# Projecting q and k of a head pair in one step, with ScalarE emptying the banks, in a convolution and attention hybrid with routed experts

## The chip, the cores and the metric

The kernel runs on one core of a Trainium2 chip. The metric is the device time in microseconds of one execution. The engines named below are TensorE (PE, with its weight loads as PEld), VectorE (DVE), ScalarE (ACT), GpSimd (POOL) and SyncE (SP).

## What is computed

The input is 8 images of 256 channels and 32 x 32 positions, so 1024 tokens of 256 features each, in float32. Three layers follow one another:

```
layer 0:  qkv = x @ w_qkv + b_qkv           8 heads of 64
          attn = softmax over i of (q_i . k_j) / 8
          x = attn @ v @ w_out + b_out + x
layer 1a: n = layer_norm(t);  t = t + softmax(n W^T n^T) n
layer 1b: n = layer_norm(t);  t = t + n + sum over the 2 best of 8 experts of
          gate * (gelu(n @ w1[e] + b1[e]) @ w2[e] + b2[e])
```

## The kernel before

The eight images are called batches. For each, `layer0` runs the attention of layer 0, `attend` the attention of layer 1, `normed` the normalisation and the router's logits. The tokens of batches 0 to 6 are scattered by expert into a DRAM table (`dispatch`) and go through `experts` in blocks after `layer0` of batch 7; batch 7 goes through all experts in `dense`.

The change lies in the head loop of `layer0`. The 8 heads form 4 pairs g. Of each pair the loop takes 8 blocks j of 128 keys, so there are 32 steps, written (g,j) below. A step consists of these parts, and TensorE gets them in this order:

- `score` makes the scores of a block of keys against 1024 queries, for head h and half n of the queries, as two 64 x 64 matmuls (psc, L399). Each head's scores take one pair of PSUM banks from the pool `ps_big`, which has three pairs. Of head 1 the second half is left to the next step.
- `first_max` and `soften` (L414, L426, L436): VectorE finds the maximum of each half, ScalarE takes the exponential with its sum. `divide` scales the values with the sums (L447).
- `gather_values` multiplies exponentials with values (po, L467) for the block two steps back (LAG), in two turns of four 64 x 64 matmuls. After the last block of a pair ScalarE copies the two accumulators to `res` (L486). The accumulators of the next pair are in the same two banks.

The first pair's q and k come from `Begin`, before the loop. Those of pair g+1 are made inside the loop by `project` (L300): four 128 x 128 matmuls into a pair of banks for q at one step and for k at another, emptied by VectorE with bias and scale (L290, in `evict`; the ScalarE form is L287). The places are listed in `PROJECT`: (0,3) and (0,5), then (g,1) and (g,5) for g = 1 and 2. At the step (3,2), the one change of pair that has no projection before it, the flag `late` puts the first turn of value products behind the scores.

The routing of the previous batch (`gates` and `dispatch`, on VectorE, with two counting matmuls, L752 and L753, into a third pair of banks `pcn`) is a generator. `share` resumes it, each time up to its next `yield`. It is resumed at step (0,0), at the places of `PROJECT`, and from (1,6) on at each step for one scatter (L804, GpSimd). In batch 0 there is nothing to route. `plan` computes on VectorE which block belongs to which expert (L830 to L879), once, behind the last eviction of batch 7 in VectorE's order, which is at (2,5).

The order on each engine is drawn up by a scheduler from dependencies; `issue_after` adds an edge on one engine alone, without a wait, and `declare_no_dep` removes a dependency that a pair of banks would give.

Of the kernel before, what the change touches and what calls it, by code (L numbers as in the profile page):

```python
# [10 lines left out]
F32 = mybir.dt.float32  # L11
I32 = mybir.dt.int32
AF = mybir.ActivationFunctionType
# [6 lines left out]
def kernel(  # L20
# [23 lines left out]
    nc = tc.nc  # L44
    P = 128
    B, C, S = x.shape
    E, D, FF = w1.shape
# [3 lines left out]
    NCC = C // P  # L51
    NT = S // P
    NH2 = S // 512
    NPAIR = INNER // P
# [20 lines left out]
    def big(name):  # L75

        return ps_big.tile([P, 1024], F32, tag="big", name=name)
# [216 lines left out]
    def project(b, xT, g, t, scalar=False):  # L294

        pq = big(f"pqk_{b}_{g}_{t}")
        dst = two.tile([P, S], F32, tag=f"qk{t}", name=f"qk{t}_{b}_{g}")
        for n in range(NH2):
            for cc in range(NCC):
                mm = nc.tensor.matmul(  # L300
                    pq[:, ts(n, 512)],
                    wqkv[:, cc, t, ts(g, P)],
                    xT[:, cc, ts(n, 512)],
                    start=(cc == 0),
                    stop=(cc == NCC - 1),
                )
                if n > 0:

                    tc.declare_no_dep(mm.ins, evicted[b, g, t].ins, reason="the other bank")
            evicted[b, g, t] = evict(dst[:, ts(n, 512)], pq[:, ts(n, 512)], g, t, scalar)  # L310
        return dst

    class Begin:


# [54 lines left out]
    def layer0(b, xT, begun, routing):  # L370
# [9 lines left out]
        steps = [(g, j) for g in range(NPAIR) for j in range(NT)]  # L380
        LAG = 2

        PROJECT = [(0, 3), (0, 5)]
        PROJECT += [(g, j) for g in range(1, NPAIR - 1) for j in (1, 5)]
        FIRST_SCATTER = PROJECT[3]
        seconds, turned = {}, {}

        relay = nc.gpsimd if b == 0 else nc.sync
        pss, firsts, nmaxes, exps, sums, vss = {}, {}, {}, {}, {}, {}
        po = None  # L390

        def score(at, h, n):
            g, j = steps[at]
            q, k = qks[g]
            if n == 0:
                pss[at, h] = big(f"psc_{b}_{g}_{j}_{h}")
            r = slice(h * DK, (h + 1) * DK)
            for c in range(2):
                mm = nc.tensor.matmul(  # L399
                    pss[at, h][ts(c, DK), ts(n, 512)],  # L400
                    k[r, j * P + c * DK : j * P + (c + 1) * DK],
                    q[r, ts(n, 512)],
                    start=True,
                    stop=True,
                )
                if n == 1:

                    tc.declare_no_dep(mm.ins, firsts[at, h].ins, reason="the other bank")
# [7 lines left out]
            )  # L416
            nmaxes[at, h] = nmax

        def soften(at, h):

            g, j = steps[at]
            ps = pss.pop((at, h))
            if h == 0:
                sums[at] = small.tile([P, 2], F32, tag="sums", name=f"sums_{b}_{g}_{j}")
            nmax = small.tile([P, 1], F32, tag="nmax", name=f"nmax_{b}_{g}_{j}_{h}")
            seconds[h] = nc.vector.tensor_scalar(  # L426
                scrap,
                ps[:, ts(1, 512)],
                -1.0,
                nmaxes.pop((at, h)),  # L430
                ALU.mult,
                ALU.min,
                accum_out=nmax,
            )
            ex = expp.tile([P, 1024], F32, tag="exps", name=f"ex_{b}_{g}_{j}_{h}")
            nc.scalar.activation(  # L436
                ex, ps, AF.Exp, bias=nmax, scale=1.0, accum_out=sums[at][:, h : h + 1]
            )
            exps[at, h] = ex

# [14 lines left out]
        def gather_values(at, turn):  # L455


            nonlocal po
            g, j = steps[at]
            if j == 0 and turn == 0:  # L460
                po = [acc(f"po_{b}_{g}_{n}") for n in range(NH2)]
            past = dict(turned)
            for half in range(2):
                keys = ts(half, DK)
                n = (half + turn) % 2
                for h in range(2):
                    mm = nc.tensor.matmul(  # L467
                        po[n][ts(h, DK), :],
                        vss[at][keys, h, :],
                        exps[at, h][keys, ts(n, 512)],  # L470
                        start=(j == 0 and turn == 0),
                        stop=(j == NT - 1 and turn == 1),
                    )
                    if h == 0 and (j > 0 or turn > 0):
                        tc.add_manual_dep(mm.ins, past[1 - half].ins.name, BEHIND)

                turned[half] = relay.nop()
                tc.add_manual_dep(turned[half].ins, mm.ins.name, BEHIND)
            if turn == 0:
                return mm  # L480
            vss.pop(at)
            for h in range(2):
                exps.pop((at, h))
            if j == NT - 1:
                for n in range(NH2):
                    nc.scalar.copy(res[:, g, ts(n, 512)], po[n])  # L486
            return mm

        last = len(steps) - 1
        def share(behind=None):  # L490

            try:
                routing.send(behind)
            except StopIteration:
                pass

        for at in range(last + LAG + 1):
            g, j = steps[min(at, last)]

            late = at > LAG and steps[at - LAG][1] == 0 and (g, j - 1) not in PROJECT  # L500
            if at <= last:
                score(at, 0, 0)
            if 0 < at <= last + 1:
                score(at - 1, 1, 1)
                soften(at - 1, 1)
            if at >= LAG and not late:
                gather_values(at - LAG, 0)
            if at <= last:

                with tc.issue_after(seconds[1].ins) if 1 in seconds else nullcontext():  # L510
                    first_max(at, 0)
                score(at, 0, 1)
                score(at, 1, 0)
                soften(at, 0)
                with tc.issue_after(seconds[0].ins):
                    ahead = divide(at - 1) if at > 0 else seconds[0]
                with tc.issue_after(ahead.ins):
                    first_max(at, 1)
            elif at == last + 1:
# [136 lines left out]
    def gates(b, lT):  # L656
# [82 lines left out]
    def dispatch(b, n2, l, group):  # L739
# [13 lines left out]
        nc.tensor.matmul(pcn[:, NT * E : 2 * NT * E], ones, flat, start=True, stop=True)  # L753
# [59 lines left out]
    def plan(group):  # L813


        with tc.issue_after(evicted[B - 1, NPAIR - 1, 1].ins):
            return plan_blocks(group)

    def plan_blocks(group):
        n, nb, cap = group.n, group.nb, group.cap  # L820
        counts = group.counts
        steps = cap // BR
# [56 lines left out]
        nc.vector.tensor_copy(w_at[:, :nb], hi)  # L879

        group.first = first
        return row_at, w_at

    def places(group):

# [22 lines left out]

    def experts(group):
        n = group.n  # L910
        row_at, w_at = plan(group)

        wbs_x = [*wbs, one.tile([P, WROW], F32, tag="v", name="wb_x")]

# [343 lines left out]
```

## Time and profile before

| | us |
|---|---|
| median of three runs | 2485.18 (2483.05 to 2487.45) |
| profiled execution, whole time | 2485.58 |
| profiled execution, span on the core | 2483.9 |
| granted TensorE clock, mean | 0.988 |
| head loop of batch 3, window 788 to 930: TensorE busy | 140.16 of 142 |
| the same window: VectorE, ScalarE busy | 115.26, 82.54 |

The profile is of one execution. Its timeline has the start and the duration of each instruction in microseconds from the start of the span, then engine, line, operation, output and inputs, and in brackets how long the engine had stood idle and what released it. Rows of single instructions are merged into xN, some matmul records are missing, and a matmul in float32 shows as two records. The releaser is inferred from semaphores, so a name in brackets is the event that came last and need not be the cause.

### The profile page before, as it was taken

To read this page: it belongs to the slowest core of one execution; us is meant where nothing else is said; L and a number is where in the kernel's file an instruction comes from. 1 tells how busy PE (TensorE), PEld (TensorE's weight loads), DVE (VectorE), ACT (ScalarE), POOL (GpSimd) and SP (SyncE) were. 2 spreads that over 40 slices of the span, in tenths; PEclk is the share of its full clock that TensorE was granted. 3 is DMA by queue.
4 is the path that set the end of the run, shared out by engine and by line. 5 is a ranking of instruction groups with operands and counts; after the bars stand their busy time and mean duration, and the time that the engine had idled before them with its cause. 6 is when DMAs were issued, how large, how long until landed. Compare 5 with 4: busy or idle time off the path is not lost.

```text
span 2483.9 us, 37112 instructions
## 1 busy us (share of the span) xinstructions
PE 2405.0 (97%) x14015; PEld 1310.7 (53%) x14015; DVE 1564.7 (63%) x3738; ACT 888.4 (36%) x1491; POOL 388.6 (16%) x383
## 2 busy tenths in 40 slices
PE   9999999999999999999999999999999999997789
PEld 3356434653465346533653365336633788865456
DVE  5874687468746875687568845885588643335434
ACT  2641355135512561255125612561255222211212
POOL 0000001000100010002000200020002354443461
PEclk9999999999999999999999999999999999998899
DMA  7993001000100000000000000000001466652352
GB/s 282 385 370 76 35 10 43 1 18 10 43 1 18 10 28 16 18 8 29 18 17 6 31 17 18 4 33 1 18 4 62 130 213 224 212 161 85 116 185 81
DMA packets 82556, 188.22 MB, mean 76 GB/s; under 512 B 13993, under 2 KB 23881, under 8 KB 80585
## 3 DMA queue, kind: packets, MB, share of 16 engines
q1 hardware_dynamic: 57368, 118.65, 13.4%
q0 software_dynamic: 25008, 67.20, 8.7%
q8 instruction: 111, 1.82, 0.3%
q14 instruction: 69, 0.56, 0.1%
HBM read 100.49 MB, written 110.90 MB: 85 GB/s over the span
## 4 chain that ended last, share of the span: by engine, by line
PE 78%; DVE 4%; ACT 2%; issue 1%; another core or an unknown queue 1%; DMA 1%; ACTq 0%; POOL 0%; DVEq 0%; SPq 0%; POOLq 0%
PE psc L399 15%; PE po L467 15%; PE py L617 8%; PE pqk L300 8%; PE ps L591 6%; PE ph L945 4%; PE pr L557 4%; PE pe L970 4%; PE pv L336 3%; PE pdy L1152 2%; PE px L576 2%; PE pdh L1128 2%; PE pa L610 2%; ACT ex L436 1%
## 5 line engine op out<-in xcount | busy, mean ns | idle before, releaser
L436 ACT ACTIVATE ex<-psc,nmax 128x1024 f32<-128x1024 f32 x512 | 570.2, 1114 | 472.2 <-DVE scrap L426 371.3
L399 PE MATMUL psc<-qk,qk 64*64 64x512 f32 x4096 | 568.2, 593 | 7.3 <-ACT ex L436 7.2
L467 PE MATMUL po<-ex,vs 64*64 64x512 f32 x4096 | 558.4, 591 | 5.4 <-DVE vs L447 4.1
L426 DVE TENSOR_SCALAR_CACHE_REDUCE scrap<-psc,nmax 128x512 f32<-128x512 f32 x512 | 384.5, 751 | 99.4 <-PE psc L399 72.4
L414 DVE TENSOR_REDUCE nmax<-psc 128x1 f32<-128x512 f32 x512 | 350.8, 685 | 12.0 <-PE psc L399 12.0
L399 PEld LDWEIGHTS psc<-qk,qk 64*64 64x64 f32 x4096 | 174.8, 132 | 299.5 <-issue 148.9
L467 PEld LDWEIGHTS po<-ex,vs 64*64 64x64 f32 x4096 | 166.7, 132 | 285.1 <-issue 97.6
L617 PE MATMUL py<-n,aT 128*128 128x256 f32 x1024 | 244.4, 393 | 18.0 <-DVE aT L612 13.2
L300 PE MATMUL pqk<-xT,wqkv 128*128 128x512 f32 x512 | 235.0, 602 | 5.4 <-ACT ex L436 5.2
L617 PEld LDWEIGHTS py<-n,aT 128*128 128x128 f32 x1024 | 195.9, 195 | 83.3 <-DVE aT L612 51.0
L804 POOL DMA_INDIRECT rows<-n,d_at x112 | 108.9, 972 | 828.6 <-DVE nmax L414 824.3
L591 PE MATMUL ps<-nT,xa 128*128 128x512 f32 x512 | 236.5, 592 | 0.0
L602 ACT ACTIVATE ex<-ps,nmax 128x1024 f32<-128x1024 f32 x64 | 71.3, 1114 | 354.7 <-DVE nmax L599 345.7
L734 POOL TENSOR_TENSOR t<-t,n 128x2048 f32<-128x2048 f32 x8 | 36.2, 4531 | 947.0 <-issue 680.5
L622 DVE SCALAR_TENSOR_TENSOR t<-py,rs,t 128x256 f32<-128x256 f32 x64 | 31.0, 484 | 233.9 <-PE py L617 207.8
L300 PEld LDWEIGHTS pqk<-xT,wqkv 128*128 128x128 f32 x512 | 93.3, 190 | 133.3 <-issue 92.8
L591 PEld LDWEIGHTS ps<-nT,xa 128*128 128x128 f32 x512 | 93.6, 190 | 79.9 <-issue 73.6
L1017 POOL DMA_INDIRECT yk<-y,yat x112 | 115.6, 1032 | 126.9 <-DVE o L1049 77.5
L336 PE MATMUL pv<-wqkv,xT 128*128 128x512 f32 x256 | 119.7, 597 | 0.0
L599 DVE TENSOR_REDUCE nmax<-ps 128x1 f32<-128x1024 f32 x64 | 78.3, 1224 | 59.1 <-PE ps L591 59.1
L557 PE MATMUL pr<-wo,res 128*128 128x256 f32 x512 | 111.8, 379 | 0.0
L290 DVE TENSOR_SCALAR qk<-pqk,b_qk 128x512 f32<-128x512 f32 x100 | 73.8, 748 | 59.6 <-PE pqk L300 59.6
(191 smaller groups left out, 2430.5 us busy)
## 6 DMA issues: line engine op xcount, KB each, us to landing
rows<-wb SPq DMA_DIRECT2D x7, 8192.0 KB
y<-yb SPq DMA_DIRECT2D x63, 256.0 KB
xT<-in_x_dram SPq DMA_DIRECT2D x7, 1024.0 KB
sums<-t SPq DMA_DIRECT2D x7, 1024.0 KB
o<-sums SPq DMA_DIRECT2D x7, 1024.0 KB
out_dram<-oT SPq DMA_DIRECT2D x14, 512.0 KB
wpack<-in_L_ffn_w_dram SPq DMA_DIRECT2D x4, 1024.0 KB
wb<-in_L_ffn_w_dram SPq DMA_DIRECT2D x16, 256.0 KB
```

The source lines that it names most:

```text
L300: mm = nc.tensor.matmul(pq[:, ts(n, 512)], wqkv[:, cc, t, ts(g, P)], xT[:, cc, ts(n, 512)], start=(cc == 0), stop=(cc == NCC - 1),)
L336: nc.tensor.matmul(pv, self.xT[:, cc, ts(i, P)], wqkv[:, cc, 2, :], start=(cc == 0), stop=(cc == NCC - 1),)
L399: mm = nc.tensor.matmul(pss[at, h][ts(c, DK), ts(n, 512)], k[r, j * P + c * DK : j * P + (c + 1) * DK], q[r, ts(n, 512)], start=True, stop ...
L414: firsts[at, h] = nc.vector.tensor_reduce(nmax, pss[at, h][:, ts(0, 512)], AX.X, ALU.max, negate=True)
L426: seconds[h] = nc.vector.tensor_scalar(scrap, ps[:, ts(1, 512)], -1.0, nmaxes.pop((at, h)), ALU.mult, ALU.min, accum_out=nmax,)
L436: nc.scalar.activation(ex, ps, AF.Exp, bias=nmax, scale=1.0, accum_out=sums[at][:, h : h + 1])
L467: mm = nc.tensor.matmul(po[n][ts(h, DK), :], vss[at][keys, h, :], exps[at, h][keys, ts(n, 512)], start=(j == 0 and turn == 0), stop=(j == ...
L557: nc.tensor.matmul(pr[:, :C], res[:, g, ts(i, P)], wo[:, g, :], start=(g == 0), stop=(g == NPAIR - 1))
L591: nc.tensor.matmul(psc[:, ts(n, 512)], xa[:, ec, ts(i, P)], nT[:, ec, ts(n, 512)], start=(ec == 0), stop=(ec == NCC - 1),)
L617: nc.tensor.matmul(py[:, :D], aT[:, ts(m, P)], n1[:, m, :], start=(m == 0), stop=(m == NT - 1))
L804: scatter = nc.gpsimd.indirect_dma_start(out=view[:, :], out_offset=bass.IndirectOffsetOnAxis(ap=ats[k][:, i : i + 1], axis=0), in_=n2[:, ...
L1017: nc.gpsimd.indirect_dma_start(out=yk[:, i, k, :], out_offset=None, in_=self.group.y[:, :], in_offset=bass.IndirectOffsetOnAxis(ap=ats[k][ ...
```

## The change

A new `project_pair` makes q and k of the next pair in one step, eight matmuls into one pair of banks: q in the first and second bank, then k in the first and second, each bank emptied by ScalarE before it is written again. The dependencies between different banks are removed. `PROJECT` has three places: (0,3), (1,1) and (2,1).

The routing loses three of its `yield`s. At (0,3) the whole of `gates` runs, and the counting matmuls go into the first of the pair's banks, behind k's last matmul; the scores and the value products of the step after are ordered behind them. At (1,1) comes all the rest up to the first scatter, and the scatters run from (1,2) on. `plan` is called at (2,1) of batch 7.

The second maximum becomes a function of its own. `late` is gone; at (3,1) the flag `early` puts the exponential of head 0 behind the two copies to `res` in ScalarE's order.

```diff
+    def project_pair(b, xT, g):
+        pq = big(f"pqk_{b}_{g}")
+        dsts, left = [], []
+        for t in range(2):
+            dst = two.tile([P, S], F32, tag=f"qk{t}", name=f"qk{t}_{b}_{g}")
+            for n in range(NH2):
+                for cc in range(NCC):
+                    mm = nc.tensor.matmul(
+                        pq[:, ts(n, 512)],
+                        wqkv[:, cc, t, ts(g, P)],
+                        xT[:, cc, ts(n, 512)],
+                        start=(cc == 0),
+                        stop=(cc == NCC - 1),
+                    )
+                    for at, ins in left:
+                        if at != n:
+                            tc.declare_no_dep(mm.ins, ins, reason="the other bank")
+                left.append((n, evict(dst[:, ts(n, 512)], pq[:, ts(n, 512)], g, t, True).ins))
+            dsts.append(dst)
+        return dsts, pq, mm
...
-        PROJECT = [(0, 3), (0, 5)]
-        PROJECT += [(g, j) for g in range(1, NPAIR - 1) for j in (1, 5)]
-        FIRST_SCATTER = PROJECT[3]
+        PROJECT = [(0, 3), *((g, 1) for g in range(1, NPAIR - 1))]
...
-                for n in range(NH2):
-                    nc.scalar.copy(res[:, g, ts(n, 512)], po[n])
+                copied = [nc.scalar.copy(res[:, g, ts(n, 512)], po[n]) for n in range(NH2)]
...
-            late = at > LAG and steps[at - LAG][1] == 0 and (g, j - 1) not in PROJECT
+            early = at > LAG and j == 1 and (g, j) not in PROJECT
             if at <= last:
-                score(at, 0, 0)
+                with tc.issue_after(counted.ins) if counted else nullcontext():
+                    score(at, 0, 0)
             if 0 < at <= last + 1:
-                score(at - 1, 1, 1)
+                with tc.issue_after(counted.ins) if counted else nullcontext():
+                    score(at - 1, 1, 1)
+                second_max(at - 1, 1)
                 soften(at - 1, 1)
-            if at >= LAG and not late:
-                gather_values(at - LAG, 0)
+            if at >= LAG:
+                with tc.issue_after(counted.ins) if counted else nullcontext():
+                    gather_values(at - LAG, 0)
+                counted = None
...
                 score(at, 0, 1)
                 score(at, 1, 0)
-                soften(at, 0)
+                second_max(at, 0)
+                if not early:
+                    soften(at, 0)
...
-            if late:
-                gather_values(at - LAG, 0)
             if at >= LAG:
                 array = gather_values(at - LAG, 1)
-            project_now = at <= last and (g, j) in PROJECT
-            if at <= last and (project_now or (g, j) > FIRST_SCATTER):
+            if early:
+                with tc.issue_after(copied[0].ins), tc.issue_after(copied[1].ins):
+                    soften(at, 0)
+            if at <= last and (g, j) in PROJECT:
                 with tc.issue_after(firsts[at, 1].ins), tc.issue_after(array.ins):
                     share(firsts[at, 1])
-            if project_now:
-                if len(qks) == g + 1:
-                    qks.append([])
-                qks[g + 1].append(project(b, xT, g + 1, len(qks[g + 1])))
+                    pair, pq, mm = project_pair(b, xT, g + 1)
+                qks.append(pair)
+                if g == 0:
+                    with tc.issue_after(mm.ins), tc.issue_after(firsts[at, 1].ins):
+                        counted = share(pq)
+                if b == B - 1 and (g, j) == PROJECT[-1]:
+                    with tc.issue_after(firsts[at, 1].ins):
+                        plan(groups[0])
+            elif at <= last and (g, j) > PROJECT[1]:
+                share(firsts[at, 1])
...
-        yield
         top2, hot2 = first_of_max(rest, "g_2")
...
-        yield
-        pcn = big(f"pcn_{b}")
+        pcn = yield
...
+        yield counted
...
-        yield
         for k in range(2):
```

The pair's matmuls are L322 in the changed kernel, the counting matmuls L792 and L793, the exponentials L461, the evictions still L287.

More of the change, by code (lines that the diff above doesn't have):

```diff
@@ L389, in layer0 @@
         pss, firsts, nmaxes, exps, sums, vss = {}, {}, {}, {}, {}, {}
-        po = None
+        po, copied, counted = None, None, None
         def score(at, h, n):
@@ L417, in first_max, with second_max @@
             nmaxes[at, h] = nmax
-        def soften(at, h):
+        def second_max(at, h):
             g, j = steps[at]
-            ps = pss.pop((at, h))
-            if h == 0:
-                sums[at] = small.tile([P, 2], F32, tag="sums", name=f"sums_{b}_{g}_{j}")
             nmax = small.tile([P, 1], F32, tag="nmax", name=f"nmax_{b}_{g}_{j}_{h}")
@@ L427, in soften @@
                 scrap,
-                ps[:, ts(1, 512)],
+                pss[at, h][:, ts(1, 512)],
                 -1.0,
-                nmaxes.pop((at, h)),
+                nmaxes[at, h],
                 ALU.mult,
@@ L434, in soften @@
             )
+            nmaxes[at, h] = nmax
+        def soften(at, h):
+            g, j = steps[at]
+            if h == 0:
+                sums[at] = small.tile([P, 2], F32, tag="sums", name=f"sums_{b}_{g}_{j}")
             ex = expp.tile([P, 1024], F32, tag="exps", name=f"ex_{b}_{g}_{j}_{h}")
             nc.scalar.activation(
-                ex, ps, AF.Exp, bias=nmax, scale=1.0, accum_out=sums[at][:, h : h + 1]
+                ex,
+                pss.pop((at, h)),
+                AF.Exp,
+                bias=nmaxes.pop((at, h)),
+                scale=1.0,
+                accum_out=sums[at][:, h : h + 1],
             )
@@ L455, in gather_values @@
         def gather_values(at, turn):
-            nonlocal po
+            nonlocal po, copied
             g, j = steps[at]
@@ L492, in share @@
             try:
-                routing.send(behind)
+                return routing.send(behind)
             except StopIteration:
-                pass
+                return None
         for at in range(last + LAG + 1):
             g, j = steps[min(at, last)]
-            late = at > LAG and steps[at - LAG][1] == 0 and (g, j - 1) not in PROJECT
+            early = at > LAG and j == 1 and (g, j) not in PROJECT
             if at <= last:
-                score(at, 0, 0)
+                with tc.issue_after(counted.ins) if counted else nullcontext():
+                    score(at, 0, 0)
             if 0 < at <= last + 1:
-                score(at - 1, 1, 1)
+                with tc.issue_after(counted.ins) if counted else nullcontext():
+                    score(at - 1, 1, 1)
+                second_max(at - 1, 1)
                 soften(at - 1, 1)
-            if at >= LAG and not late:
-                gather_values(at - LAG, 0)
+            if at >= LAG:
+                with tc.issue_after(counted.ins) if counted else nullcontext():
+                    gather_values(at - LAG, 0)
+                counted = None
             if at <= last:
@@ L748, in dispatch @@
         nc.vector.tensor_add(both, hots[0], hots[1])
-        yield
-        pcn = big(f"pcn_{b}")
+        pcn = yield
         flat = both.rearrange("p i e -> p (i e)")
         nc.tensor.matmul(pcn[:, : NT * E], before, flat, start=True, stop=True)
-        nc.tensor.matmul(pcn[:, NT * E : 2 * NT * E], ones, flat, start=True, stop=True)
+        counted = nc.tensor.matmul(pcn[:, NT * E : 2 * NT * E], ones, flat, start=True, stop=True)
         cn = small.tile([P, 2, NT, E], F32, tag="d_cn", name=f"d_cn_{b}", bufs=1)
         nc.vector.tensor_copy(cn.rearrange("p t i e -> p (t i e)"), pcn[:, : 2 * NT * E])
+        yield counted
         per = small.tile([P, E, NT], F32, tag="d_per", name=f"d_per_{b}", bufs=1)
@@ L813, in plan @@
     def plan(group):
-        with tc.issue_after(evicted[B - 1, NPAIR - 1, 1].ins):
-            return plan_blocks(group)
-    def plan_blocks(group):
         n, nb, cap = group.n, group.nb, group.cap
@@ L881, in plan_blocks @@
         group.first = first
-        return row_at, w_at
+        group.where = row_at, w_at
     def places(group):
@@ L910, in experts @@
         n = group.n
-        row_at, w_at = plan(group)
+        row_at, w_at = group.where
         wbs_x = [*wbs, one.tile([P, WROW], F32, tag="v", name="wb_x")]
```

## The prediction

> **What bounds the kernel now.** I read the page's busy shares, then the chain, then the chip's timeline of single steps, because the answer must come from places where TensorE waits.
>
> ```profile
> PE 2405.0 (97%) x14015; PEld 1310.7 (53%) x14015; DVE 1564.7 (63%) x3738; ACT 888.4 (36%) x1491; POOL 388.6 (16%) x383
> L399 PE MATMUL psc<-qk,qk 64*64 64x512 f32 x4096 | 568.2, 593 | 7.3 <-ACT ex L436 7.2
> L290 DVE TENSOR_SCALAR qk<-pqk,b_qk 128x512 f32<-128x512 f32 x100 | 73.8, 748 | 59.6 <-PE pqk L300 59.6
> ```
>
> TensorE is the bound: busy 97%, 78% of the chain. Only time in which it stands still or works inefficiently inside the eight head loops (142 us each) is to be had; the matmuls themselves stay. Since an overlapping busy row hides small gaps, I use a clock of my own: the distance from the first exponential (h = 0) of one step to that of the next. A plain step takes 3.43 us, almost everywhere. What a step takes beyond that, and beyond its extra matmuls, is loss. Batch 3, a step with one projection:
>
> ```profile
> 862.04 1.11 ACT L436 ACTIVATE ex<-psc,nmax 128x1024 f32<-128x1024 f32 x1 [0.35 <-DVE rs L445]
> 865.37 0.30 PEld L300 LDWEIGHTS pqk<-xT,wqkv 128*128 128x128 f32 x2 [0.81 <-ACT ex L436]
> 865.47 1.11 ACT L436 ACTIVATE ex<-psc,nmax 128x1024 f32<-128x1024 f32 x1 [0.34 <-DVE rs L445]
> 867.39 0.75 DVE L290 TENSOR_SCALAR qk<-pqk,b_qk 128x512 f32<-128x512 f32 x1 [1.01 <-PE pqk L300]
> 869.00 0.21 PEld L399 LDWEIGHTS psc<-qk,qk 64*64 64x64 f32 x8 [0.76 <-issue]
> 872.69 1.11 ACT L436 ACTIVATE ex<-psc,nmax 128x1024 f32<-128x1024 f32 x1 [0.48 <-DVE rs L445]
> ```
>
> 862.04 to 865.47 is the plain step, 865.47 to 872.69 (7.22 us) the step with a projection. The weight loads inside it start every 0.43 us, eight of them: 3.44 us of work. So 7.22 - 3.43 - 3.44 = **0.35 us** is lost at each entry and exit. It looks like a wait for ScalarE's exponential (0.81), but that one began at 863.92 and took 1.11, and its accumulator was read by 865.12, 0.25 us before the load: the gap lies where the 64*64 tiles turn into 128*128 and back.
>
> The dearer places, found by the same clock:
>
> ```profile
> 828.90 1.11 ACT L436 ACTIVATE ex<-psc,nmax 128x1024 f32<-128x1024 f32 x1 [0.35 <-DVE rs L445]
> 830.16 0.30 PEld L300 LDWEIGHTS pqk<-xT,wqkv 128*128 128x128 f32 x2 [0.84 <-ACT ex L436]
> 837.48 1.11 ACT L436 ACTIVATE ex<-psc,nmax 128x1024 f32<-128x1024 f32 x1 [0.48 <-DVE rs L445]
> ```
>
> Step (1,1) takes 8.58, which is 1.36 more than 7.22: the counting matmuls (loads at 828.80 and 829.02) took the free pair of banks, and the projection waits for the exponential that began at 828.90 to give back its own. Seven batches have this; batch 0 routes nothing.
>
> ```profile
> 900.52 1.11 ACT L436 ACTIVATE ex<-psc,nmax 128x1024 f32<-128x1024 f32 x1 [0.35 <-DVE rs L445]
> 901.62 1.06 ACT L486 COPY res<-po 128x512 f32<-128x512 f32 x2
> 903.89 1.11 ACT L436 ACTIVATE ex<-psc,nmax 128x1024 f32<-128x1024 f32 x1
> 908.47 1.11 ACT L436 ACTIVATE ex<-psc,nmax 128x1024 f32<-128x1024 f32 x1 [0.48 <-DVE rs L445]
> ```
>
> Steps (3,1) and (3,2), the one change of pair without a projection: 7.95 for 6.87, 1.08 lost, in every batch.
>
> ```profile
> 1887.55 1.11 ACT L436 ACTIVATE ex<-psc,nmax 128x1024 f32<-128x1024 f32 x1 [0.34 <-DVE rs L445]
> 1896.50 1.11 ACT L436 ACTIVATE ex<-psc,nmax 128x1024 f32<-128x1024 f32 x1 [1.45 <-DVE rs L445]
> 1902.24 1.09 PE L399 MATMUL psc<-qk,qk 64*64 64x512 f32 x8 [2.55 <-ACT ex L436]
> 1902.47 1.11 ACT L436 ACTIVATE ex<-psc,nmax 128x1024 f32<-128x1024 f32 x1 [0.28 <-DVE rs L445]
> ```
>
> Batch 7, (2,5) and (2,6): 8.95 and 5.97 instead of 7.22 and 3.43, together 4.3 lost, because the plan's VectorE work (L830 to L879) sits among the second maxima.
>
> ```profile
> 299.86 1.11 ACT L436 ACTIVATE ex<-psc,nmax 128x1024 f32<-128x1024 f32 x1 [7.61 <-PE po L467]
> ```
>
> Batch 1 alone: pair 0 takes 42.94 us where batch 2 takes 36.74, so 6.2 lost. Its value products stand behind the projection in TensorE's order, and ScalarE waits for them (7.61) to free a buffer of exponentials.
>
> **What the Trainium skill says.** (1) TensorEngine Tiling (Array Packing), Key Properties: "Mode switching requires drain". The trace agrees; the price here is the 0.35. (2) ScalarE: Activation LUTs, Table sets: identity and copy are in every set, so an eviction between exponentials needs no load. The trace agrees for the copies of L486, which stand between exponentials without one; for identity there it shows nothing. (3) PSUM — Partial Sum Buffer, PSUM bank collisions: engines on different banks run clean, on one bank they must be kept apart. Agrees: loads go on every 0.43 us while VectorE empties the first bank.
>
> **The change part by part.**
>
> *A. Six projections become three pairs.* 24 entries fewer in eight batches, 24 x 0.35 = **8.4**. Does the shared pair of banks take it back? Count from the pair's first weight load. VectorE's first eviction began at 2.02 (867.39 - 865.37); the next results come 1.72 apart, at 3.74, 5.46, 7.18. ScalarE's identity takes 0.69 (L287, 128x512). At (0,3) it has finished its exponential by about 1.4; at (1,1) and (2,1) also two copies (1.06, begun at 1.21), free at 2.27. So q's first bank is empty at 2.71 or 2.96, and k needs it at 3.44; the second at 4.43, needed at 5.16. Slack 0.48 and 0.73: no stall. The last eviction ends at 7.87; the next exponential is ready at 5.64 + 3.44 = 9.08, and the scores that take this pair of banks come at 4.97 + 3.44 = 8.41. Hidden, with 0.5 to spare. If the cover fails, each 0.1 us costs 2.4 in all. VectorE loses 96 evictions (96 x 0.748 = 72 us), ScalarE gains 96 x 0.687 = 66 us; neither engine is the bound, so I cost that at nothing. Bounds: 3 to 9.
>
> *B. Counting in the pair's own first bank, at (0,3).* No third pair of banks is taken, so the 0.84 wait goes. The two matmuls stay, about 0.5 of the 1.36. Their input must be ready: the gates' 20 small VectorE instructions took 2.3 us in the first portion and 1.6 in the second; begun at about 1.0 they end near 4.9, before 6.9, when the pair is through. VectorE's copy of the counts ends near 8.1, before the second maximum behind it can start (8.6). 7 x 0.86 = **6.0**; bounds 4 to 6.7. The rest of the routing (1.4 us of VectorE for the rows, L757 to L774, and 2.4 for the slots, L786 to L796) goes under the pair at (1,1), a span of 7. Its 16 scatters (0.97 each on GpSimd, 16% busy) come four steps earlier; SP's order doesn't change.
>
> *C. At (3,1) the copies go before the exponential, and the value products return to their place.* The last product ends about when the exponential would start, so two copies delay it by some 0.9. The scores that want its banks start as soon as they are free even now, so TensorE loses 0.5 to 0.9. ScalarE, 2.6 busy of 3.43 in a step, catches up in two steps. I take 0.8 in place of 1.08: 8 x 0.28 = **2.2**. Bounds -2.4 to 6.4, since the trace has no such order.
>
> *D. Plan at (2,1) of batch 7.* Its twenty instructions sum to 6.74 us. With VectorE's evictions gone it is free from 1.0 (end of the first maximum) to 8.2 (the second maximum's earliest start): 7.2. I leave 0.2 exposed: **4.1**; bounds 2.8 to 4.3. The weight fetches behind the plan move four steps earlier on POOL, past one scatter; the first expert's inputs were already in before the loop ended.
>
> *E. Batch 1.* In the changed kernel's order TensorE still does two steps' scores ahead, but three groups of value products (0.86 each) stand before the pair, not behind it. The last ends some 1.5 later than a regular step would; with relay waits of up to 1 us I put the loss at 2.3, not 6.2: **3.9**; bounds 1.5 to 5.5.
>
> Sum: 8.4 + 6.0 + 2.2 + 4.1 + 3.9 = 24.6. Outside the head loops both orders are the same. The profiled execution (span 2483.9, 2485.58 in all) lies 0.4 above the median 2485.18, so the sum applies to it: 2485.2 - 24.6 = **2460.6**. With all low ends 9 is left (2476), with all high ends 32 (2453).
>
> **Rivals.**
>
> *R1, smaller gain (25%):* the wait on ScalarE is real and C costs. A gives 3, C loses 2.4, the rest 11: 2473. For it: the view names ScalarE before each projection. Against: 0.25 us lies between its end and the load.
>
> *R2, slower (5%):* the two banks don't run apart, so TensorE stands at each of three bank changes of a pair until the eviction just begun is over: 0.30 to the result, 0.69, some 1.0 each, 24 x 3 = 72, less 24.6: 2532. It decides from 1.02 us of stall per pair (24.6/24). Against: the loads every 0.43 now, and in the changed order k's first matmul waits for ScalarE, q's second for nothing.
>
> *R3, no change (5%):* the change doesn't do what it says: k waits for both of q's evictions (4.43 against 3.44, 1.0 x 24 = 24 lost): 2485.
>
> **Numbers.** A measurement of this kernel can tell about 0.2%, 5 us, from no change. Main case 65%: 2460.6, with 2452 to 2470 from the bounds. R1 25%, R2 and R3 5% each. Faster 0.90 (main and R1), same 0.05 (R3), slower 0.05 (R2). The range, 2451 to 2474, adds the best sum and R1.
>
> **What would show it.** (0,3) at about 11.2 us, (1,1) and (2,1) at 10.7, (3,1) and (3,2) together 7.7, batch 7's (2,1) within 0.3 of batch 6's, pair 0 of batch 1 some 2 above batch 2. No table load beside L287; about 124 instructions of L287, 4 of L290. Wrong, if TensorE's loads of the pair show gaps over 0.43 with ScalarE's identity as releaser, or the sum over a middle batch falls by less than 1 us.

## The result and the profile after

The changed kernel takes 2464.67 us (median of 6 runs, 2456.93 to 2466.82); the kernel before, run beside it, 2486.31 (6 runs, 2479.73 to 2489.04). The ratio is 0.9909, 95% interval 0.989 to 0.9929: 21.6 us faster. The profiled execution of the changed kernel took 2459.43 us, its span is 2457.7; that is 5 us under its median, so totals are compared by medians and places by the clock of steps.

The page of the changed kernel, the lines that answer to those shown of before:

```profile
PE 2386.2 (97%) x14015; PEld 1323.8 (54%) x14015; DVE 1497.3 (61%) x3642; ACT 953.5 (39%) x1587; POOL 391.1 (16%) x383
L420 PE MATMUL psc<-qk,qk 64*64 64x512 f32 x4096 | 574.7, 592 | 4.3 <-ACT ex L461 4.3
L287 ACT ACTIVATE qk<-pqk,b_qks 128x512 f32<-128x512 f32 x124 | 85.6, 691 | 96.1 <-PE pqk L322 79.8
```

VectorE has 67 us less, ScalarE 65 more, and TensorE is still the bound at 97%. As before, these shares do not tell where the time went; the clock does. The 31 distances between the first exponentials of a batch, summed over eight batches, were 1077.6 us and are 1057.7: 19.9 gained inside the head loops, so nearly all of it. The timeline of batch 3, step (2,1), a pair without anything else:

```profile
856.46 1.11 ACT L461 ACTIVATE ex<-psc,nmax 128x1024 f32<-128x1024 f32 x1 [0.34 <-DVE rs L475]
859.47 0.19 PEld L322 LDWEIGHTS pqk<-xT,wqkv 128*128 128x128 f32 x1 [0.24 <-ACT qk L287]
862.47 0.19 PEld L322 LDWEIGHTS pqk<-xT,wqkv 128*128 128x128 f32 x1 [0.24 <-issue]
863.42 0.21 PEld L420 LDWEIGHTS psc<-qk,qk 64*64 64x64 f32 x8 [0.76 <-issue]
867.12 1.11 ACT L461 ACTIVATE ex<-psc,nmax 128x1024 f32<-128x1024 f32 x1 [0.48 <-DVE rs L475]
```

The step takes 867.12 - 856.46 = 10.66, that is 3.43 for the plain step, 16 x 0.43 for the pair and 0.35. The line at 859.47 is the first of the loads that wait for an eviction of ScalarE by name; its 0.24 of idle time is what every load of the pair behind the first shows, so TensorE does not stand where k begins.

Step (0,3) of the same batch, where the counting matmuls (now L792) are:

```profile
792.51 1.11 ACT L461 ACTIVATE ex<-psc,nmax 128x1024 f32<-128x1024 f32 x1 [0.34 <-DVE rs L475]
796.95 0.22 DVE L789 TENSOR_TENSOR d_both<-g_hot,g_hot 128x64 f32<-128x64 f32 x1
797.86 0.69 ACT L287 ACTIVATE qk<-pqk,b_qks 128x512 f32<-128x512 f32 x1 [1.03 <-PE pqk L322]
798.52 0.19 PEld L322 LDWEIGHTS pqk<-xT,wqkv 128*128 128x128 f32 x1 [0.24 <-issue]
799.57 0.69 ACT L287 ACTIVATE qk<-pqk,b_qks 128x512 f32<-128x512 f32 x1 [1.03 <-PE pqk L322]
800.31 0.30 PEld L792 LDWEIGHTS pqk<-d_both,before 128*128 128x128 f32 x2 [1.61 <-ACT qk L287]
804.60 1.11 ACT L461 ACTIVATE ex<-psc,nmax 128x1024 f32<-128x1024 f32 x1 [0.48 <-DVE rs L475]
```

12.09, which is 1.43 more than the pair alone. The input of the counting matmuls is there at 797.17, the bank that they write (the first) is empty at 797.86 + 0.69 = 798.55, the next load was due at 798.52 + 0.43 = 798.95. The load begins at 800.31, when the eviction that began at 799.57 is over. That eviction empties the **second** bank, which the counting matmuls do not touch.

The change of pair at (3,1), batch 3:

```profile
887.72 1.11 ACT L461 ACTIVATE ex<-psc,nmax 128x1024 f32<-128x1024 f32 x1 [0.34 <-DVE rs L475]
891.15 1.07 ACT L515 COPY res<-po 128x512 f32<-128x512 f32 x2 [0.34 <-PE po L497]
892.11 1.13 ACT L461 ACTIVATE ex<-psc,nmax 128x1024 f32<-128x1024 f32 x1
894.62 1.11 ACT L461 ACTIVATE ex<-psc,nmax 128x1024 f32<-128x1024 f32 x1 [0.20 <-DVE rs L475]
898.56 1.11 ACT L461 ACTIVATE ex<-psc,nmax 128x1024 f32<-128x1024 f32 x1 [0.28 <-DVE rs L475]
```

The copies now stand before the exponential at 892.11. The three distances are 4.39, 2.51 and 3.94, together 10.84 for 10.30: 0.54 lost in place of 1.08. The plan in batch 7, step (2,1): its last instruction (L905) ends before the next exponential needs VectorE, and the step takes 10.65, as in the other batches.

```profile
1854.68 1.11 ACT L461 ACTIVATE ex<-psc,nmax 128x1024 f32<-128x1024 f32 x1 [0.34 <-DVE rs L475]
1861.45 0.19 DVE L905 CAST row_at<-p_lo 128x63 int32<-128x63 f32 x1
1865.33 1.11 ACT L461 ACTIVATE ex<-psc,nmax 128x1024 f32<-128x1024 f32 x1 [0.48 <-DVE scrap L444]
```

In batch 1, (0,3) takes 14.40 us, 2.3 more than in batch 2.

### The profile page after: what moved, and what is told of

Its sections match the earlier page's. It is cut to its first block, busy times and chain, and to the rows that moved or that the text cites. A ratio compares the mean times of both kernels' runs of the same rounds, so it can differ in the third digit from the quotient of the medians.

```text
span 2457.7 us, 37143 instructions
## 1 busy us (share of the span) xinstructions
PE 2386.2 (97%) x14015; PEld 1323.8 (54%) x14015; DVE 1497.3 (61%) x3642; ACT 953.5 (39%) x1587; POOL 391.1 (16%) x383
## 4 chain that ended last, share of the span: by engine, by line
PE 90%; DVE 3%; ACT 2%; issue 2%; DMA 1%; another core or an unknown queue 1%; SPq 0%; ACTq 0%; DVEq 0%; POOLq 0%
PE psc L420 18%; PE po L497 18%; PE py L659 9%; PE ps L633 7%; PE pqk L322 7%; PE pr L599 4%; PE pv L359 4%; PE ph L981 4%; PE pe L1006 4%; PE pdy L1188 2%; PE pdh L1164 2%; PE px L618 2%; PE pqk L300 2%; PE pa L652 2%
## 5 line engine op out<-in xcount | busy, mean ns | idle before, releaser
L461 ACT ACTIVATE ex<-psc,nmax 128x1024 f32<-128x1024 f32 x512 | 570.5, 1115 | 304.3 <-DVE scrap L444 221.8
L420 PE MATMUL psc<-qk,qk 64*64 64x512 f32 x4096 | 574.7, 592 | 4.3 <-ACT ex L461 4.3
L497 PE MATMUL po<-ex,vs 64*64 64x512 f32 x4096 | 570.2, 591 | 3.8 <-DVE vs L477 3.0
L420 PEld LDWEIGHTS psc<-qk,qk 64*64 64x64 f32 x4096 | 179.8, 132 | 279.9 <-ACT ex L461 133.0
L497 PEld LDWEIGHTS po<-ex,vs 64*64 64x64 f32 x4096 | 175.3, 132 | 273.4 <-DVE vs L477 80.3
L322 PE MATMUL pqk<-xT,wqkv 128*128 128x512 f32 x384 | 171.2, 599 | 0.0
L322 PEld LDWEIGHTS pqk<-xT,wqkv 128*128 128x128 f32 x384 | 71.0, 190 | 99.9 <-issue 77.8
L287 ACT ACTIVATE qk<-pqk,b_qks 128x512 f32<-128x512 f32 x124 | 85.6, 691 | 96.1 <-PE pqk L322 79.8
```

The costliest lines, as they stand in the source:

```text
L322: mm = nc.tensor.matmul(pq[:, ts(n, 512)], wqkv[:, cc, t, ts(g, P)], xT[:, cc, ts(n, 512)], start=(cc == 0), stop=(cc == NCC - 1),)
L420: mm = nc.tensor.matmul(pss[at, h][ts(c, DK), ts(n, 512)], k[r, j * P + c * DK : j * P + (c + 1) * DK], q[r, ts(n, 512)], start=True, stop ...
L461: nc.scalar.activation(ex, pss.pop((at, h)), AF.Exp, bias=nmaxes.pop((at, h)), scale=1.0, accum_out=sums[at][:, h : h + 1],)
L497: mm = nc.tensor.matmul(po[n][ts(h, DK), :], vss[at][keys, h, :], exps[at, h][keys, ts(n, 512)], start=(j == 0 and turn == 0), stop=(j == ...
```

## The experiments

All of them are read by the clock. Between the two profiles of the changed kernel 246 of the 248 distances agree within 0.02 us (the other two, in batch 7, differ by 0.10 and 0.27), while totals spread over several us. Five versions were run once (old change of pair, exponential first, routing and plan uncovered, and both splits); of them only the clock is used. In the sessions of the experiments the kernel before took 2448.5 to 2450.4 us, and the changed kernel, run again, 2428.59 (ratio 0.9913, 0.99 to 0.9927). Its head loops came out at 1057.4 us, 0.3 from the first time.

> The changed kernel itself, on the same chip as the last version, to compare the two. Every step as in its first trace (head loops together 1057.7 us), 0.991 of the kernel before.

| kernel | head loops, us | against | difference |
|---|---|---|---|
| before | 1077.6 | | |
| changed | 1057.4 | before | -20.2 |
| counting matmuls released | 1050.0 | changed | -7.3 |
| the same, order of batch 1 held | 1048.2 | released | -1.8 |
| VectorE empties the banks | 1076.4 | changed | +19.1 |
| banks tied | 1134.9 | changed | +77.5 |
| old change of pair | 1061.4 | changed | +4.0 |
| exponential first, products in place | 1064.1 | changed | +6.8 |
| routing and plan uncovered | 1089.0 | changed | +31.7 |
| pairs alone | 1097.2 | before | +19.7 |
| split by half a group of scores | 1078.8 | released | +28.7 |
| split by a whole group | 1056.8 | order held | +8.6 |

### The counting matmuls released from the other bank

```diff
+        for ins in others:
+            tc.declare_no_dep(mm.ins, ins, reason="the other bank")
+            tc.declare_no_dep(counted.ins, ins, reason="the other bank")
```

> The changed kernel, with the two counting matmuls of (0,3) released from the evictions of the pair's other (second) bank; they still wait for k's first bank. Order of all engines unchanged. Theory (the counting matmuls stand for the last eviction, of the bank they do not touch): their weight load moves up from 1.8 us behind the pair's last load to about 0.45 behind it, step (0,3) of batches 2 to 7 falls from 12.08 us to 11.0 (10.8 to 11.2), 7 times 1.1 = 7 to 8 us less in the head loops than the changed kernel. Rival (it is the gates' input or the copy of the counts that is late, or the releaser is only the event that came last): (0,3) stays at 12.0 to 12.1 and the time is the changed kernel's.

Timeline of this kernel, batch 3, (0,3):

```profile
796.45 0.19 PEld L322 LDWEIGHTS pqk<-xT,wqkv 128*128 128x128 f32 x1 [0.24 <-issue]
796.88 0.19 PEld L792 LDWEIGHTS pqk<-d_both,before 128*128 128x128 f32 x1 [0.24 <-issue]
797.51 0.69 ACT L287 ACTIVATE qk<-pqk,b_qks 128x512 f32<-128x512 f32 x1 [1.03 <-PE pqk L322]
801.48 1.11 ACT L461 ACTIVATE ex<-psc,nmax 128x1024 f32<-128x1024 f32 x1 [0.47 <-DVE rs L475]
```

`others` are the two evictions of the second bank. The counting load follows the last load of the pair by 0.43, before the second bank's last eviction has even begun (797.51). (0,3) falls from 12.09 to 11.04 in every batch from 2 on, and to 13.33 in batch 1. Seven times 1.05 is the whole difference: the wait was for the wrong bank. What remains, 11.04 - 10.66 = 0.38, is what the two matmuls cost. The time is 2422.47 us, ratio to before 0.9894 (0.9878 to 0.9911).

### The dependency between the pair's banks left in

```diff
-                    for at, ins in left:
-                        if at != n:
-                            tc.declare_no_dep(mm.ins, ins, reason="the other bank")
...
-                        counted = share(pq)
+                        counted = share(pq) or mm
+                else:
+                    counted = mm
```

The second part only holds TensorE's order behind the pair.

> The changed kernel with the dependencies between a pair's two banks left in, and the same order of all instructions (TensorE's order behind the pair held by hand). Theory (the banks do run apart, and that is what makes one pair of banks enough): each of the three bank changes in a pair now stands until the eviction just begun is over, 0.43 to the result and 0.69 for the eviction, about 1.15 each; steps (0,3), (1,1) and (2,1) 3.4 us longer (10.66 to 14.1), 24 times 3.4 = 82 us more, about 2546. Rival (the banks are slowed by each other anyway, or TensorE is bound elsewhere): less than 1 us per step, under 24 us more.

Timeline, batch 3, (2,1), the second bank of q:

```profile
894.04 0.71 ACT L287 ACTIVATE qk<-pqk,b_qks 128x512 f32<-128x512 f32 x1
894.80 0.30 PEld L322 LDWEIGHTS pqk<-xT,wqkv 128*128 128x128 f32 x2 [1.76 <-ACT qk L287]
```

The load starts when the eviction ends. Steps (1,1) and (2,1) take 13.94, 3.28 more, so 1.09 for each of three bank changes; 24 pairs make 77.5 us, and the kernel is slower than before (2504.1 us, ratio 1.0225, 1.0205 to 1.0246). The size of R2 was right (1.0 estimated); what kept it away is the released dependency.

### VectorE empties the banks

```diff
-                left.append((n, evict(dst[:, ts(n, 512)], pq[:, ts(n, 512)], g, t, True).ins))
+                left.append((n, evict(dst[:, ts(n, 512)], pq[:, ts(n, 512)], g, t, False).ins))
```

> The changed kernel with VectorE emptying the pair's banks in place of ScalarE (the same four evictions in the same step). Theory A (VectorE has room, only the routing and the plan ahead of it matter): batch 0 unchanged (10.65 per pair step); (0,3) of the others within 0.3, because the gates end about when q's first result is there; (1,1) 0 to 1.5 longer; (2,1) of batch 7 about 4 to 5 longer behind the plan; in all 5 to 14 us more than the changed kernel. Rival (ScalarE is what carries the change, VectorE being at 63% would hold every pair): each of the 24 pair steps 0.5 or more longer, 12 us more even without the plan.

Batch 0 stays at 10.65. In the others (0,3) takes 13.46 and (1,1) 12.10, 1.4 more each, and (2,1) of batch 7 takes 12.13. Both theories were wrong in part: only steps with routing or the plan pay, but (0,3) pays as well. Batch 3, (0,3):

```profile
801.16 0.74 DVE L290 TENSOR_SCALAR qk<-pqk,b_qk 128x512 f32<-128x512 f32 x1
801.96 0.30 PEld L322 LDWEIGHTS pqk<-xT,wqkv 128*128 128x128 f32 x2 [1.87 <-DVE qk L290]
```

q's first result is due 2.0 after the first load (797.21), at 799.2; VectorE comes to it at 801.16, because fourteen instructions of the gates stand ahead. I had the gates end about when q's first result is there; their last one ends at 802.58, 3.4 later. The kernel takes as long as before (2447.95 us, ratio 0.9998, 0.9989 to 1.0007). So VectorE's share of the whole span, 63% before, was no sign of room in these steps: **with VectorE emptying the banks, the rest of the change brings nothing.**

### Routing and plan in plain steps

```diff
+                    if (g, j) != (1, 1):
                         share(firsts[at, 1])
...
+            elif at <= last and (g, j) == (1, 3):
+                with tc.issue_after(firsts[at, 1].ins), tc.issue_after(array.ins):
+                    share(firsts[at, 1])
+            elif at <= last and (g, j) > (1, 3):
                 share(firsts[at, 1])
+                if b == B - 1 and (g, j) == (2, 4):
+                    with tc.issue_after(firsts[at, 1].ins):
+                        plan(groups[0])
...
```

The scatters then begin at (1,4), and `plan` is no longer called at (2,1).

> The changed kernel with two portions of VectorE work moved from under a pair into plain steps: the second portion of the routing from (1,1) to (1,3) (about 3.8 us, seven batches), and the plan from (2,1) to (2,4) of batch 7 (6.7 us). Theory (the pair's long step is what hides them, not VectorE's freed time): (1,3) and (1,4) lose 2.5 to 3.5 us together, 17 to 25 in all; (2,4) to (2,6) of batch 7 lose 4.3 to 6.5. Rival (VectorE without evictions has room everywhere): less than 1 us at each place.

Timeline of this kernel, step (1,3) of batch 4:

```profile
1096.48 1.11 ACT L461 ACTIVATE ex<-psc,nmax 128x1024 f32<-128x1024 f32 x1 [0.34 <-DVE rs L475]
1102.99 1.11 ACT L461 ACTIVATE ex<-psc,nmax 128x1024 f32<-128x1024 f32 x1 [0.47 <-DVE rs L475]
```

(1,3) takes 6.44 to 6.51 (6.22 in batch 2) for 3.43: 3.0 us lost, in seven batches. In batch 7, (2,4) takes 8.47 and (2,5) 4.76: 6.4 lost for a plan of 6.7. Most of VectorE's work goes straight into the length of the step, because TensorE stands meanwhile (2.69 us behind the routing in batch 4).

The total came out just above the expectation, because in three places the step after such a stretch is long as well: (1,4) in batches 1 and 5 loses another 1.7 and 1.3, and 1.3 of the 6.4 are lost at (2,5) of batch 7. TensorE works there at a lower granted clock: 0.69, 0.59 and 0.65. In batch 5 its weight loads come 0.86 apart for over three us in place of 0.43, after it had stood 2.68 us. In batch 4 it had stood 2.69, and the granted clock stays at 1.00; what decides between the two these traces do not show.

### The pairs alone

The kernel before, with `project_pair` at the three new places, the routing's four portions and the plan where they were.

> The kernel before with part A alone: three pairs at (0,3), (1,1) and (2,1), emptied by ScalarE. The routing keeps its old portions at (0,3), (0,5), (1,1), (1,5) and the plan its place at (2,5), of which (0,5), (1,5) and (2,5) are now plain steps; the counting matmuls keep a pair of banks of their own. Theory (the parts hold each other up: each portion needs a long step above it): batch 0 gains 1.05; in the others the pairs gain 1.05, but the uncovered portions cost about 0.8 at (0,5) and 1.6 at (1,5), and the plan 6.4 in place of 4.3, so the head loops together come out 0 to 12 us longer than the 1077.6 of the kernel before. Rival (the parts add up): 8.4 us shorter than the kernel before, at once.

Batch 0 gains 1.07 in its pair steps and those that lost a projection. In the others (0,5) takes 4.61, (1,5) 5.56, and (2,5) to (2,7) of batch 7 lose 6.1; (1,1) with the counting matmuls in their own banks takes 12.02, 1.36 over the pair. The kernel is slower than before: 2467.55 us, ratio 1.0069 (1.0054 to 1.0085). **The parts do not add up**: two portions of routing were hidden by projections that the pairs take away. The loss of 19.7 us is above the 12 expected at most. Of it 5.0 come at (1,6) in batches 4, 5 and 7 (5.0 to 5.2 for 3.43), where the granted clock is 0.65 to 0.67; at (2,6) of batch 7 it is 0.52.

### What an entry and an exit costs

To see whether 0.35 is a change of tiles or a wait, I split the pair in the middle by scores that come anyway (at first `between` is `score(at, 1, 1)`, which then falls away in the next step; k's matmuls are ordered behind it):

```diff
+            if t == 1:
+                with tc.issue_after(mm.ins):
+                    behind = between()
...
```

> The kernel with the counting matmuls released, and the pair's eight matmuls split in the middle: the second scores of head 1 (two 64*64 matmuls, which otherwise open the next step) stand between q and k. No work is added; TensorE's tiles change twice more per pair. Theory (part A: an entry and exit costs 0.35 us of TensorE's time, whoever waits): pair steps 0.35 longer (10.66 to 11.0), 24 times 0.35 = 8.4 us more in the head loops. Rival (the 0.35 was a wait for ScalarE's exponential at the entry, as the releaser named in the profile says): nothing more, as no exponential is waited for in the middle.

The pair steps rose by 1.19, not by 0.35. That left two readings: a change of tiles costs 1.19, or the two score matmuls now run alone, without the other head's two that stand beside them otherwise, and take the time of four (3.43 / 4 = 0.86). The second version puts the whole group of four there (`between` is `score(at + 1, 0, 0)` and `score(at, 1, 1)`):

> The version with counting released and batch 1's order held, with the pair split in the middle once more, now by a whole group of scores (head 0 of the next step and head 1 of this one, four 64*64 matmuls that run beside each other), so that nothing loses its partner. Theory (an entry and exit costs 0.35, and the 1.19 of the first split was that plus 0.86 for scores without a partner): (1,1) and (2,1) go from 10.66 to 11.0. Rival (a change of tiles costs 1.19): they stay at 11.85. Rival (the cost at an entry is a wait for the exponential): 10.66.

(1,1) and (2,1) take 11.01 to 11.03 in all batches but 2 and 5 (where (2,1) is 0.07 longer with and without the split), in place of 10.66: 0.35. Timeline of that kernel, (2,1) of batch 3, the two entries and the scores between them:

```profile
855.54 0.30 PEld L326 LDWEIGHTS pqk<-xT,wqkv 128*128 128x128 f32 x2 [0.81 <-ACT ex L468]
859.17 0.21 PEld L426 LDWEIGHTS psc<-qk,qk 64*64 64x64 f32 x8 [0.76 <-ACT qk L288]
860.19 0.30 PEld L326 LDWEIGHTS pqk<-xT,wqkv 128*128 128x128 f32 x2 [0.81 <-ACT qk L288]
```

Idle time 0.81 at both; the profile names ScalarE's exponential at one and an eviction at the other. Whatever event came last is named, the gap is the same: it belongs to the change of tiles. The eviction named at the second had begun at 859.28 and was over at 859.97, 0.22 before the load; the exponential at the first was over 0.25 before it. A load that does wait follows much closer: 0.05 behind the eviction with the banks tied (894.75, 894.80) and at the counting matmuls (800.26, 800.31). And at (0,3) of batch 1 of the changed kernel the same 0.81 stands before the first load (293.32) with no releaser named at all.

The group of four takes 1.02 from its first load to the next load of the pair (859.17 to 860.19). In the first split the two matmuls without partners take 1.01 (870.15 to 871.16), so the second reading of the 1.19 holds. How the 0.35 divides between entry and exit is not shown.

### The change of pair

Back to the kernel before at this place (`early` off, `late` as it was):

> The changed kernel with the change of pair at (3,1) and (3,2) as in the kernel before: the exponential ahead of the copies, the first value products behind the scores. Theory (the order is what the gain of part C came from): (3,0) to (3,2) together lose 1.08 again in place of 0.55, everything else unchanged, 8 times 0.5 = 4 us more. Rival (the smaller loss came from VectorE being freer or from the pairs): the sum stays at 10.85.

(3,0) to (3,2) lose 1.08 again. And with `early = False` alone:

> The changed kernel with only the flag early off: at (3,1) the exponential of head 0 again stands ahead of the two copies to res, the value products stay in their new, regular place. Theory (the two edits of part C need each other: value products in the regular place pay only if the copies come first): the products of the new pair wait for copies that begin 1.1 to 1.3 us later; (3,0) to (3,2) lose 1.2 to 1.9 us in place of 0.55, 5 to 11 us more in all. Rival (the place of the products alone makes the gain, the copies' place is idle): 0.55 lost as now.

They lose 1.39. The products in their regular place, without the copies in front, wait for the copies, which begin behind the exponential. Timeline, batch 3:

```profile
895.07 1.06 ACT L515 COPY res<-po 128x512 f32<-128x512 f32 x2
895.70 0.19 PEld L497 LDWEIGHTS po<-ex,vs 64*64 64x64 f32 x4 [1.79 <-ACT res L515]
```

So the products' new place by itself would be a loss of 0.3 against the kernel before; the copies' new place by itself was not run.

### The order of batch 1

```diff
-                with tc.issue_after(counted.ins) if counted else nullcontext():
+                behind = counted or (array if b == 1 else None)
+                with tc.issue_after(behind.ins) if behind else nullcontext():
                     score(at, 0, 0)
```

> The changed kernel with the counting matmuls released from the other bank's evictions, and besides in batch 1 alone the first scores of a step queued behind the value products of the step before, which gives batch 1 the order on TensorE that batches 2 to 7 have. Theory (batch 1's surplus is that order and nothing else): its (0,3) falls from 13.33 to 11.04, its 31 steps from 133.06 to 130.8, all other batches unchanged: 2.3 us less than with the counting matmuls released alone. Rival (the semaphores that pass through SyncE, which packs weights by DMA at that time, are late in fact): the loss moves to other steps and the batch keeps 133.

(0,3) falls from 13.33 to 11.06, (0,2) rises from 3.39 to 3.83: 1.8 gained of the 2.3. So most of batch 1's surplus was the order; the 0.4 at (0,2) stays open. This kernel, which has the counting matmuls released as well, takes 2419.15 us (ratio 0.987, 0.9854 to 0.9887), and again

> The changed kernel with the counting matmuls released and batch 1's order held, once more, beside the changed kernel. Theory: 1048.2 us in the head loops, 9.5 less than the changed kernel; total 0.3 to 0.45% under it, ratio to the kernel before about 0.987.

2419.30 us beside the changed kernel's 2428.59, ratio to before 0.9871 (0.9856 to 0.9886). It is the fastest version: 9.3 us under the changed kernel, 9.2 of them in the head loops.

## Why the prediction was right, and where it was wrong

The predicted time was 2460.6, the measured one 2464.67, within the range. By its own sum the head loops should have gained 24.6 and gained 20.2. Term by term, from the clock:

| term | predicted | measured |
|---|---|---|
| A, pairs | 8.4 | 24 x 0.36 = 8.6 |
| B, counting | 6.0 | 7 x (1.36 - 1.43) = -0.5 |
| C, change of pair | 2.2 | 8 x 0.5 = 4.0 |
| D, plan | 4.1 | 4.3 |
| E, batch 1 | 3.9 | 6.2 - 2.3 = 3.9 |
| sum | 24.6 | 20.3 |

A, right. The 0.35 per entry and exit is a price of the change of tiles: the split by a whole group shows it without any wait, 8.6 us for 24. That fits what the Trainium skill states, that a change of the tiling mode drains TensorE (TensorEngine Tiling (Array Packing), Key Properties); the traces show the price, not the draining itself. The slack between bank and eviction held: behind the first, no load of a pair stands. What the term left out is that it needs the rest of the change: the pairs alone lose 19.7 us.

**B failed**, in the sentence "No third pair of banks is taken, so the 0.84 wait goes". The prediction followed two events that the counting matmuls need, their input and the end of the pair, but not the third, the release of the tile that they write. Its own count held the number: the last eviction ends at 7.87 after the first load, where the matmuls were due at 6.9. The dependency between banks was lifted for the pair's matmuls only; the counting matmuls wait for every reader of the pair of banks. One wait of about 1 us took the place of another, and releasing it brought 7.3 us. With it released the term comes to 7 x (1.36 - 0.38) = 6.9, so the rest of its reasoning was sound.

C, right in mechanism, mis-sized: 0.54 lost in place of 0.8. The exponential of (3,1) comes at 892.11, 0.96 late; the next, at 894.62, is only 0.04 late, so ScalarE catches up within one step, not two; what remains at 898.56 is the 0.54 that TensorE lost, the low end of the 0.5 to 0.9. On the clock this shows in (3,0) as well, so that (3,1) and (3,2) alone (6.45) are not the 7.7 foretold; the sum to compare is that of all three.

D and E, right. The plan lies under the pair wholly. It needs the long step, since in plain steps it costs 6.4 us, and VectorE's freed time, since under a pair that VectorE empties (2,1) of batch 7 takes 12.13, 1.5 more than in the other batches. In batch 1 the loss is 2.3, as estimated, and mostly TensorE's order.

The other signs: 124 instructions of L287 and 4 of L290 as foretold; (1,1) and (2,1) 10.66; (0,3) 12.09 and not 11.2 (B). Because B brought nothing, the sum over batch 3 falls by only 1.36 (133.47 to 132.11), near the 1 us below which the prediction would have called itself wrong. ScalarE loads its tables as often as before (35 times) and at none of the evictions, which agrees with the skill (ScalarE: Activation LUTs, Table sets). R1 did not happen: the releaser named at the entry was not the cause. R3 neither, as far as the pair's own matmuls go; its mechanism, a wait for the eviction of the other bank, was real at the counting matmuls.

That the time lay within the range although B failed is in part luck: the 6.5 us that B missed are less than half of the range's width, and C brought 1.8 more than its term. That the total gain (21.6 by medians) is nearer to the prediction than the head loops' 20.2 means nothing: the rest lies within the spread of the totals.

## What to carry to other kernels

For every instruction that is moved into a shared buffer, list all that it waits for: its inputs, its place in the queue, and each reader of the buffer that the framework takes for a conflict, even of a part that it does not touch. A portion of work on a second engine can cost nothing under a long step of the bounding engine and nearly its whole length elsewhere (here nothing under a pair, 3.0 and 6.4 us in plain steps); before shortening or merging such steps, note what they cover. Where the wait named in the profile ends well before the instruction starts, vary the order until another releaser is named: if the gap stays, it was never that wait.

## What had not been expected of the hardware

Two 64*64 score matmuls without the other head's two beside them cost 1.19 - 0.35 = 0.84 us of TensorE's time, about as much as a group of four takes in the plain step (0.86).

A wait can cost more than its own length: after TensorE had stood 1.9 to 2.8 us, the granted clock of the next step was 0.59 to 0.69 in some batches and 1.00 in others, and where it was low the step lost another 1.3 to 1.7 us (routing and plan uncovered; pairs alone). The traces show that the one follows the other, not why some batches are spared.

The same kernel took 2464.67 us in one session and 2428.59 in another, with head loops that agree within 0.4 us: in the two profiles, whose spans are 2457.7 and 2426.1, the first exponential of batch 7's last step began at 1910.91 and at 1910.63. The whole difference lies behind it, in the experts and the dense part, where the granted clock in the window from 2200 to 2420 us was 0.88 in one profile and 0.95 in the other. The kernel before shows the same 0.88 there in the first session, and fell from 2486.31 to 2450.44, so the difference is one of sessions and not of the change; its cause is open.
